# A graph-attention layer's opening in three-chunk steps: one product per chunk for h, r and s, first tile woven in, and the bias moved to x

## Chip, core and metric

One NeuronCore of a Trainium2 chip runs the whole program. The metric is the device time of one execution in microseconds (us); lower is better. PE is TensorE, DVE is VectorE, ACT is ScalarE, POOL is GpSimd, and SP is the SyncE, whose queue issues most DMAs. ACT issues some DMAs too, on a queue of its own.

## What is computed

Everything is float32. `x` has 3327 rows of 128, `adj` is 3327 x 3327 with entries 0 and 1 and ones on the diagonal. Two layers follow each other, each with a residual sum and a layer norm.

```
# layer 0
h = x @ W.T + b;  s = h @ a_s;  r = h @ a_r
e = leaky_relu(adj * s + adj * r.T, 0.2)
x1 = layernorm(x + softmax(where(adj > 0, e, -9e15), axis=1) @ h)
# layer 1: 8 features per head, 128 heads, each attends over all 3327 rows
q, k, v = (x1 @ W.T).reshape(128, 3327, 8)  for Wq, Wk, Wv
a = softmax(q @ k.T / sqrt(128) + adj + adj, axis=2)
out = layernorm(x1 + (a @ v).reshape(3327, 1024) @ Wo.T)
```

## The kernel before

**The long part, layer 1.** The 128 heads are taken in 32 groups of four. For a group, the 3327 query columns are taken in 7 blocks of 476, and the 3327 keys in 26 chunks of up to 128 (key row `p*26 + i` stands on partition `p` of chunk `i`). A block has 26 rounds, so a group has 182 and the kernel 5824. In a round PE computes scores for four head-and-chunk pairs (L135, tiles `scb` from `k4b` and `q4b`), DVE adds the adjacency to some (L1013) and ACT takes the exponential (L843), while for every third chunk ACT takes the exponential directly (L1010) and POOL multiplies by a factor made of the adjacency (L1011). Four rounds later PE multiplies with the values (L813, `av` from `e` and `v4b`). Adjacency tiles `at` hold three chunks (a stretch) and are loaded three stretches ahead by `want_adj` (L776); `make_factor` (L799) turns a tile's first chunk into POOL's factor in the first blocks.

**Between groups.** `open_group` (L735) loads the next group's `k4b` (four loads, one per head) and `v4b` (three loads) from DRAM. It is called when 28 rounds of the old group are left (`OPEN`, L852), and the seven loads are spread over these 28 rounds (L983 to L989). Before the call, `finish_to` (L949) forces whatever is left of the layer-0 tile whose rows the group needs, in one piece.

**Layer 0.** It is worked by row tiles of 128, 26 of them, by `layer0(t)` (L250). A tile needs its adjacency columns in three loads of chunks (`a`, `load_adj`), the exponentials of s for its rows (`trow`, from a table `td` in DRAM), and per chunk: weights `w` on DVE (`weigh`), their mask by `a` on POOL (`mask`, tiles 1 and up), and one PE product into an accumulator of 129 columns (`product`; the last column gives the softmax denominator). The operand `hsb` holds h scaled by an exponential of r. After the 26 products a chain follows: divide and add x (`finish`, L329), variance, an inverse root by Newton steps, scaling, a transpose to `x1T`, then q, k and v projections of 512 columns (tile 0) or 128 columns (the others), each split or copied and stored to DRAM (`qT`, `kT`, `vd`). `count` counts zeros and ones in the adjacency on DVE (L313). Tiles 1 to 25 are not done at once: their steps are put between the rounds of layer 1, a few per round, by `work_tensor` and `work` (L925, L932), in two rows: `main` (products, chain) and `aside` (weights, masks, counts). `work` runs at most one POOL step and one or no DVE step per round.

**The opening.** Before the first round everything that all tiles share and all of tile 0 is done in line (L612 to L705). In order: x is loaded; 26 transposes give `xT` (L650); seven products of 476 columns give h transposed, and DVE adds the bias b (L658); seven products give s, ACT takes the exponential and each row piece is stored to `td` (L663); 26 products with an identity that has `a_r` as a 129th column turn h back and give r (L674); two exponentials of r over all chunks (L682); POOL scales `hsb` in three pieces (L686). Then tile 0: `spread` copies a row of s to all partitions by a product (L284), 26 weights (L297), 26 products (L182), the chain. Its stores go to SP one step after they are made (`issue` and `tick`, L238), q first, then k, then v. The counts and the load of `wo` come last. Then `group` 0 is opened: q and k loads alternate between SP and ACT, v on ACT; three adjacency tiles are wanted; and tile 1's adjacency is loaded (L957 to L969). `trow` of tile 1 is loaded when the rounds have begun.

[...]

Of the kernel before, what the change touches and what calls it, by code (L numbers as in the profile page):

```python
# [8 lines left out]
F32 = mybir.dt.float32  # L9
# [38 lines left out]
def kernel(  # L48
# [76 lines left out]
    identr = const.tile([P, P + 1], F32, name="identr")  # L125
    ident = identr[:, :P]
# [17 lines left out]
    def special():  # L144
        with ExitStack() as sx, tc.manual_schedule(engines=ALL):
# [15 lines left out]
            hsb = keep.tile([P, NT, D + 1], F32, name="hsb")  # L161
            vbs = [keep.tile([P, 512 // H, H1], F32, name=f"vb{n}") for n in range(2)]
# [4 lines left out]
            ear = keep.tile([P, NT], F32, name="ear")  # L167
# [82 lines left out]
            def layer0(t, side=True, trow=None, bank=bank):  # L250
# [31 lines left out]
                def spread():  # L282
                    s["b"] = bank()
                    nc.tensor.matmul(s["b"][:, :r], one_row, trow[:, :r], start=True, stop=True)  # L284

                def weigh(n, c0, c1):
                    i0 = CH[n][0]
                    if c0 == i0:
                        s["w"][n] = bgw.tile([P, CW, 3 * T3], F32, name="w")
                    for i in range(c0, c1):  # L290
                        w, e = s["w"][n][:, i - i0, :r], er[:, i : i + 1]
                        if side:

                            w = s["w"][n][:, i - i0, :].rearrange("p (a b) -> p a b", b=T3)
                            nc.vector.tensor_scalar(w, s["t"][:, :, :T3], e, None, op0=ALU.max)  # L295
                        else:
                            nc.vector.scalar_tensor_tensor(  # L297
                                w, s["b"][:, :r], e, s["a"][n][:, i - i0, :r], op0=ALU.max, op1=ALU.mult
                            )
# [17 lines left out]
                def product(i):  # L317
# [9 lines left out]
                    )  # L327

# [50 lines left out]
                def halves(dst, c, scale):  # L379
# [13 lines left out]
                    if o + QW == 512:  # L393
                        h0 = c // 512 * 4
                        for half, sb in ((0, hi), (1, lo)):
                            at = (h0 * 2 + half if dst is qT else half * H + h0) * G + t * P * D
                            for p0, p1 in _cut(r):
                                issue(
                                    lambda at=at, sb=sb, p0=p0, p1=p1: nc.sync.dma_start(
# [5 lines left out]
                def values(c):  # L405
# [5 lines left out]
                    if c % 512 + QW == 512:  # L411
                        for p0, p1 in _cut(r):
                            at = ((t * P + p0) * D + c // 512 * (512 // H)) * H1
                            issue(
                                lambda at=at, p0=p0, p1=p1: nc.sync.dma_start(
# [6 lines left out]
                for w, dst, sc in ((wq, qT, half_scale), (wk, kT, 1.0)):  # L422
# [8 lines left out]
                main, aside = [("x", load)], [("r", load_row)] if side else [("p", spread)]  # L431
                loads = [("x", lambda n=n: load_adj(n)) for n in range(len(CH))]
                counts = []
                for n, (i0, i1) in enumerate(CH):
# [12 lines left out]
                    main.append(("n", ("W", q0 + n, 3)))  # L447
                    main += [("p", lambda i=i: product(i)) for i in range(i0, i1)] + [("t", ("P", q0 + n))]
# [163 lines left out]
            nc.vector.memset(dens, 1.0)  # L612
            nc.vector.memset(even, 0.0)
            with ExitStack() as st:
                pro = st.enter_context(tc.tile_pool(name="st_sb", bufs=1))
                pps = st.enter_context(tc.tile_pool(name="st_ps", bufs=5, space=bass.MemoryType.PSUM))
                w0 = pro.tile([P, D], F32, name="w0")
                bcol = pro.tile([P, 1], F32, name="bcol")
                ascol = pro.tile([P, 1], F32, name="ascol")
                xsb = pro.tile([P, NT, D], F32, name="xsb")  # L620
                xT = pro.tile([P, P * NT], F32, name="xT")
                hT = pro.tile([P, P * NT], F32, name="hT")
                for p0, p1 in _cut(FP):
                    nc.sync.dma_start(xsb[p0:p1], x[p0 * NT : p1 * NT, :].rearrange("(p i) d -> p i d", i=NT))
                nc.sync.dma_start(xsb[FP:P, :REST, :], x[FP * NT :, :].unsqueeze(0))
                nc.scalar.dma_start(w0, w0T)
                nc.scalar.dma_start(bcol, b0)
                nc.scalar.dma_start(ascol, a_s)
                nc.scalar.dma_start(identr[:, P : P + 1], a_r)
                nc.gpsimd.memset(hsb[:, REST:NT, :], 0.0)  # L630
                trs = [pro.tile([1, WB], F32, name=f"tr{b}") for b in range(NBLK)]
                loads, main, aside = layer0(
                    0, side=False, trow=trs[0], bank=lambda: pps.tile([P, 512], F32, tag="mm", name="mm")
                )
                for _, u in loads + main[:1]:
                    u()
                nc.sync.dma_start(wq, wqT.rearrange("k h c -> k (h c)"))
                nc.sync.dma_start(wk, wkT.rearrange("k h c -> k (h c)"))
                nc.sync.dma_start(wv, wvT.rearrange("k c h -> k (c h)"))

                def evict(n, dst, src):
                    (nc.scalar.copy if n % 2 else nc.vector.tensor_copy)(dst, src)


                xv, hv = (v.rearrange("d (p i) -> d i p", i=NT) for v in (xT, hT))
                for n, i0 in enumerate(range(0, NT, 4)):
                    pt = pps.tile([P, 4, P], F32, tag="mm", name="pt")
                    k = min(4, NT - i0)
                    for i in range(i0, i0 + k):
                        nc.tensor.transpose(pt[:, i - i0, : kr[i]], xsb[: kr[i], i, :], ident[: kr[i], : kr[i]])  # L650
                    full = sum(kr[i] == P for i in range(i0, i0 + k))
                    if full:
                        evict(n, xv[:, i0 : i0 + full, :], pt[:, :full, :])
                    if full < k:
                        evict(n, xv[:, i0 + full : i0 + k, :FP], pt[:, full:k, :FP])
                for n, (n0, _) in enumerate(blocks):
                    ph = pps.tile([P, 512], F32, tag="mm", name="ph")
                    nc.tensor.matmul(ph[:, :WB], w0, xT[:, n0 : n0 + WB], start=True, stop=True)  # L658
                    nc.vector.tensor_scalar(hT[:, n0 : n0 + WB], ph[:, :WB], bcol, None, op0=ALU.add)

                for b, (n0, _) in enumerate(blocks):
                    pr = pps.tile([P, 512], F32, tag="mm", name="pr")
                    nc.tensor.matmul(pr[:1, :WB], ascol, hT[:, n0 : n0 + WB], start=True, stop=True)  # L663
                    nc.scalar.activation(trs[b], pr[:1, :WB], AF.Exp, scale=ALPHA - 1.0)
                    nc.scalar.dma_start(td[:, n0 : n0 + WB], trs[b])
                nc.scalar.dma_start(td[:, N:], one_row[:, : NT * P + 1 - N])

                for n, i0 in enumerate(range(0, NT, 3)):
                    pb = pps.tile([P, 512], F32, tag="mm", name="pb")[:, : 3 * (D + 1)].rearrange(
                        "p (c d) -> p c d", d=D + 1  # L670
                    )
                    k = min(3, NT - i0)
                    for i in range(i0, i0 + k):
                        nc.tensor.matmul(  # L674
                            pb[: kr[i], i - i0, :], hv[:, i, : kr[i]], identr, start=True, stop=True
                        )
                    full = sum(kr[i] == P for i in range(i0, i0 + k))
                    if full:
                        evict(n, hsb[:, i0 : i0 + full, :], pb[:, :full, :])
                    if full < k:  # L680
                        evict(n, hsb[:FP, i0 + full : i0 + k, :], pb[:FP, full:k, :])
                nc.scalar.activation(er, hsb[:, :, D], AF.Exp, scale=1.0 - ALPHA)  # L682
                nc.scalar.activation(ear, hsb[:, :, D], AF.Exp, scale=ALPHA)
                nc.gpsimd.memset(hsb[:, :, D : D + 1], 1.0)
                for i0, i1 in CH:
                    nc.gpsimd.tensor_tensor(  # L686
                        hsb[:, i0:i1, :],
                        hsb[:, i0:i1, :],
                        ear[:, i0:i1].unsqueeze(2).to_broadcast([P, i1 - i0, D + 1]),
                        op=ALU.mult,  # L690
                    )
                for u in aside:
                    if isinstance(u, list):
                        while main[1][0] != "t":
                            kind, f = main.pop(1)
                            if kind == "p":
                                f()
                        main.pop(1)
                    elif u[0] in "pd":
                        u[1]()  # L700
                for kind, f in main[1:] + sum((u for u in aside if isinstance(u, list)), []):
# [263 lines left out]
            for m in range(AHEAD):  # L965
                want_adj(m)
# [447 lines left out]
```

## Time and profile before

| | |
|---|---|
| three timed runs | 10145.96, 10146.45, 10153.09 us; median 10146.45 |
| the profiled execution | 10146.98 us, of which the span of the trace is 10145.2 |
| busy in the span | ACT 9978.5 us (98%), PE 9936.6 (98%), DVE 9373.0 (92%), POOL 9211.9 (91%) |
| DMA | 1730 MB, mean 171 GB/s |

All times below are us from the span's start. A timeline row has the start, the time, the engine and line, the operation, the tile written and the tiles read, and the number of instructions that the row merges; in brackets stands the engine's idle time before it and what ended it. PE records two instructions per float32 product and one per transpose. `PEld` are weight loads, which lie under the products. A row of the stretches has, for each engine, the busy time and the number of instructions, then the granted PE clock as a share of full speed, the busy share of the DMA engines, and GB/s. An engine name with `q` is its queue of DMA issues. An idle engine costs nothing unless it is the one that sets the pace.

### The profile page before, as it was taken

The page shows a single profiled execution, that of the slowest core. Times are in us where ns is not written, and L with a number is a line of the kernel's source. Part 1 is how long each engine was busy: PE and PEld are TensorE (multiplying, and loading weights), DVE is VectorE, ACT ScalarE, POOL GpSimd, SP SyncE. Part 2 cuts the span into 40 slices and gives each one's busy share as a digit, 9 for nine tenths or more (in the row PEclk, how much of TensorE's full clock was granted, in tenths as well). Part 3 has the DMA queues.
Part 4 walks back from the last instruction along what each step waited for, and adds up shares of the span by engine and source line. Part 5 has one row for each costly group of instructions (what it writes and reads, how often), then busy time and mean ns, then how long its engine had stood idle before and what let it go on. Part 6 is the DMA issues. An engine that isn't in the chain of part 4 may idle for free.

```text
span 10145.2 us, 212048 instructions
## 1 busy us (share of the span) xinstructions
PE 9936.6 (98%) x81993; PEld 3855.0 (38%) x81993; DVE 9373.0 (92%) x11597; ACT 9978.5 (98%) x8311; POOL 9211.9 (91%) x4395
## 2 busy tenths in 40 slices
PE   7999999999999999999999999999999999999998
PEld 3333333333333333333333333333333333333333
DVE  6999999999989999989999999999999999998887
ACT  6999999999999999999999999999999999999998
POOL 6999999999999999989999999999999999998997
PEclk8999999999999999999999999999999999999999
DMA  6655555555555555555555565555555555555553
GB/s 174 200 177 166 176 170 174 172 170 173 177 162 175 178 158 176 176 168 172 168 170 175 173 182 166 159 173 175 173 178 164 163 177 175 172 162 168 165 166 121
DMA packets 1183195, 1730.00 MB, mean 171 GB/s; under 512 B 131326, under 2 KB 1170783, under 8 KB 1177949
## 3 DMA queue, kind: packets, MB, share of 16 engines
q1 hardware_dynamic: 1180810, 1714.81, 56.4%
q8 instruction: 645, 10.57, 0.4%
q14 instruction: 377, 3.09, 0.1%
q10 hardware_dynamic: 1363, 1.53, 0.1%
HBM read 1611.93 MB, written 103.95 MB: 169 GB/s over the span
## 4 chain that ended last, share of the span: by engine, by line
PE 79%; ACT 12%; DVE 4%; issue 2%; POOL 2%; DMA 1%; SPq 0%; DVEq 0%; ACTq 0%; POOLq 0%
PE av L813 40%; PE scb L135 33%; ACT e L843 6%; ACT e L1010 6%; PE bank L224 4%; DVE e L1013 3%; POOL e L1011 2%; DVE o L822 1%; PE bank L472 0%; DMA at<-ftd 0%; DMA at<-in_adjT_dram 0%; POOL at L803 0%; PE mm L182 0%; PE pb L674 0%; DMA k4b<-kT 0%
## 5 line engine op out<-in xcount | busy, mean ns | idle before, releaser
L1011 POOL TENSOR_TENSOR e<-e,at 128x952 f32<-128x952 f32 x4032 | 8969.4, 2238 | 818.0 <-ACT e L1010 739.4
L1013 DVE TENSOR_TENSOR e<-scb,at 128x952 f32<-128x952 f32 (+1 forms) x7616 | 8417.8, 1144 | 647.3 <-PE scb L135 333.0
L843 ACT ACTIVATE e<-e 128x1904 f32<-128x1904 f32 (+2 forms) x4256 | 6886.4, 1624 | 16.3 <-DVE e L1013 15.5
L813 PE MATMUL av<-e,v4b 128*32 128x476 f32 x46592 | 5872.4, 572 | 42.1 <-DVE o L822 27.8
L135 PE MATMUL scb<-q4b,k4b 32*128 32x476 f32 (+1 forms) x23296 | 4351.5, 592 | 116.8 <-ACT e L1010 36.1
L135 PEld LDWEIGHTS scb<-q4b,k4b 32*128 32x128 f32 (+1 forms) x23296 | 2533.6, 295 | 4788.8 <-issue 2642.1
L1010 ACT ACTIVATE e<-scb 128x952 f32<-128x952 f32 x4032 | 3882.0, 963 | 67.9 <-PE scb L135 37.7
L813 PEld LDWEIGHTS av<-e,v4b 128*32 128x32 f32 x46592 | 1056.6, 108 | 1068.5 <-issue 616.1
L224 PE MATMUL bank<-hsb,w 128*32 128x129 f32 (+1 forms) x5200 | 278.0, 286 | 0.0
L313 DVE TENSOR_SCALAR_CACHE_REDUCE dump<-a 128x384 bf16<-128x384 f32 (+2 forms) x468 | 247.2, 528 | 0.6
L295 DVE TENSOR_SCALAR w<-trow,er 128x129 f32<-128x129 f32 x650 | 201.1, 338 | 13.6 <-DMA trow<-td 13.6
L304 POOL TENSOR_TENSOR w<-w,a 128x384 f32<-128x384 f32 (+3 forms) x225 | 207.3, 921 | 0.1
L224 PEld LDWEIGHTS bank<-hsb,w 128*32 128x32 f32 (+1 forms) x5200 | 102.4, 108 | 148.3 <-issue 147.9
L822 DVE COPY o<-av 128x476 f32<-128x476 f32 x224 | 146.0, 652 | 7.5 <-PE av L813 6.7
L389 DVE SCALAR_TENSOR_TENSOR lo<-bank,hi 128x128 fp32r<-128x128 f32 (+1 forms) x400 | 116.6, 292 | 13.8
L386 DVE TENSOR_SCALAR hi<-bank 128x128 fp32r<-128x128 f32 (+1 forms) x400 | 112.2, 281 | 0.0
L224 PE MATMUL bank<-wv,x1T 128*32 128x128 f32 x1600 | 86.1, 287 | 5.6 <-DVE vb L408 5.6
L224 PE MATMUL bank<-wo,ot 128*32 128x128 f32 (+1 forms) x1664 | 88.8, 290 | 0.4 <-DVE ot L481 0.4
L224 PE MATMUL bank<-wq,x1T 128*32 128x128 f32 x1600 | 85.2, 285 | 0.0
L224 PE MATMUL bank<-wk,x1T 128*32 128x128 f32 x1600 | 85.2, 285 | 0.0
L472 PE MATMUL bank<-identr,o 128*128 128x128 f32 (+1 forms) x234 | 54.6, 308 | 11.0 <-DMA o<-oT 8.3
L408 DVE COPY vb<-bank 128x128 f32<-128x128 f32 (+1 forms) x200 | 56.2, 281 | 6.4 <-PE bank L224 6.4
(110 smaller groups left out, 667.5 us busy)
## 6 DMA issues: line engine op xcount, KB each, us to landing
at<-in_adjT_dram SPq DMA_DIRECT2D x1736, 476.0 KB
at<-ftd SPq DMA_DIRECT2D x1953, 238.0 KB
q4b<-qT SPq DMA_DIRECT2D x1788, 29.8 KB
k4b<-kT SPq DMA_DIRECT2D x126, 415.9 KB
at<-in_adjT_dram SPq DMA_DIRECT2D x217, 208.2 KB
at<-in_adjT_dram SPq DMA_DIRECT2D x56, 714.0 KB
a<-in_adjT_dram SPq DMA_DIRECT2D x50, 504.0 KB
ftd<-at SPq DMA_DIRECT2D x63, 238.0 KB
```

Of the source, the lines that this page charges most:

```text
L135: nc.tensor.matmul(dst, k4[32 * j : 32 * j + H4, i::NT], q4[32 * j : 32 * j + H4, :nb], start=True, stop=stop,)
L224: nc.tensor.matmul(dst[c0:c1], w[:, c0:c1], mov, **kw)
L295: nc.vector.tensor_scalar(w, s["t"][:, :, :T3], e, None, op0=ALU.max)
L304: nc.gpsimd.tensor_tensor(w, w, s["a"][n][:, c0 - i0 : c1 - i0, :r], op=ALU.mult)
L313: nc.vector.tensor_scalar(z, a, float(k), None, op0=ALU.is_equal, op1=ALU.add, accum_out=even[:, t, at : at + 1])
L389: nc.vector.scalar_tensor_tensor(lo[:r, o : o + QW], s["b"][:r, :QW], scale, hi[:r, o : o + QW].bitcast(F32), op0=ALU.mult, op1=ALU.subtract,)
L813: nc.tensor.matmul(s.av[32 * j : 32 * j + 32, :], s.v4[:r, j, i * H1 : i * H1 + 32], e[:r, j, :], start=(s.left == NT - 1), stop=(s.left = ...
L822: nc.vector.tensor_copy(o4, s.av)
L843: nc.scalar.activation(e, e, AF.Exp, scale=2.0)
L1010: nc.scalar.activation(eh, z[:r, :, :WB], AF.Exp, scale=2.0)
L1011: nc.gpsimd.tensor_tensor(eh, eh, ah, op=ALU.mult)
L1013: nc.vector.tensor_tensor(eh, z[:r, :, :WB], ah, op=ALU.add)
```

## The change

- The bias leaves h. h is now `x @ W.T` alone; b is added to the tile's rows of x on POOL (`biased`), for tile 0 ahead of the chain and for each other tile ahead of its last eight products. (The softmax weights sum to one, so b passes through the weighted sum unchanged.)
- r and s become two more columns of W: `w0` gets `W.T @ a_r` and `W.T @ a_s`, by two small products at the start, and one product of 130 columns per chunk of x gives h, r and s (`linear`). b's share in r and s is put in as a bias of ACT's exponentials. ACT, not POOL, scales `hsb`, chunk by chunk.
- x is loaded in two halves, after tile 0's rows. Three chunks at a time are transposed (`turn`), multiplied a step later, weighed for tile 0, and multiplied for tile 0 two steps after that.
- Tile 0's row of s (`t0`) is computed by itself, from its transposed rows, on all partitions. The table `td` is stored by columns after the last step.
- All tiles project k, then q, then v. Tile 0's k stores stay on SP; its q and v stores are kept in a list (`held`) and issued on ACT when the whole chain has been issued; the counts come after that.
- The first three adjacency tiles are loaded early, behind the weights. At group 0 the four k loads go to SP, q and v loads to ACT. `trow` of tile 1 is loaded ahead of its adjacency, and `wo` after it.
- `OPEN` is 18 instead of 28 rounds.

The diff, cut to its core:

```diff
-                main, aside = [("x", load)], [("r", load_row)] if side else [("p", spread)]
+                main, aside = [("x", load)], [("r", load_row)] if side else []
...
+                    if i1 == NT:
+                        main.append(("m", biased))
                     main += [("p", lambda i=i: product(i)) for i in range(i0, i1)] + [("t", ("P", q0 + n))]
...
+                def biased():
+                    nc.gpsimd.tensor_tensor(s["x"][:r], s["x"][:r], brow[:r], op=ALU.add)
...
-                for w, dst, sc in ((wq, qT, half_scale), (wk, kT, 1.0)):
+                for w, dst, sc in ((wk, kT, 1.0), (wq, qT, half_scale)):
...
+                nc.scalar.dma_start(w0[:, :D], w0T)
+                nc.scalar.dma_start(acol[:, 0:1], a_r)
+                nc.scalar.dma_start(acol[:, 1:2], a_s)
+                nc.scalar.dma_start(bcol, b0)
+                nc.scalar.dma_start(brow, _ap(b0, 0, [[0, P], [1, D]]))
+                first["load"]()
...
+                for m in range(AHEAD):
+                    want_adj(m)
...
+                nc.tensor.transpose(b[:, :D], w0[:, :D], ident)
+                nc.vector.tensor_copy(w0t, b[:, :D])
+                b = mm()
+                nc.tensor.matmul(b[:, 0:2], w0t, acol, start=True, stop=True)
+                nc.tensor.matmul(b[:, 4:6], bcol.to_broadcast([P, P]), acol, start=True, stop=True)
...
+                def turn(cs):
+                    b = pps.tile([P, 4, P], F32, tag="mm", name="mm")
+                    for i in cs:
+                        nc.tensor.transpose(b[:, i - cs[0], : kr[i]], xsb[: kr[i], i, :], ident[: kr[i], : kr[i]])
+                    for i, k, r in parts(cs):
+                        nc.vector.tensor_copy(xT[:, i : i + k, :r], b[:, i - cs[0] : i - cs[0] + k, :r])
+
+                def linear(cs):
+                    b = mm()[:, : 3 * (D + 2)].rearrange("p (c d) -> p c d", d=D + 2)
+                    for i in cs:
+                        nc.tensor.matmul(b[: kr[i], i - cs[0], :], xT[:, i, : kr[i]], w0, start=True, stop=True)
+                    for i, k, r in parts(cs):
...
+                        nc.scalar.activation(
+                            er[:r, i : i + k], v[:, :, D], AF.Exp, scale=1.0 - ALPHA, bias=bias[:r, 0:1]
+                        )
...
+                    for i in cs:
+                        nc.scalar.mul(hsb[: kr[i], i, :D], b[: kr[i], i - cs[0], :D], hsb[: kr[i], i, D : D + 1])
+                    for i in cs:
+                        first["weigh"][i]()
+
+                for n in range(len(three) + 3):
+                    if n < len(three):
+                        turn(three[n])
+                    if 1 <= n <= len(three):
+                        linear(three[n - 1])
+                    if n >= 3:
+                        for i in three[n - 3]:
+                            first["product"][i]()
...
+                for f in first["chain"]:
+                    f()
+                    tick(True)
+                for f in held:
+                    f()
+                for f in first["count"]:
+                    f()
...
-            OPEN = min(28, total // 2)
+            OPEN = min(18, total // 2)
...
             for j in range(HG):
-                engine = nc.scalar if j % 2 else nc.sync
-                queries[1](j, engine)
-                group[2][j](engine=engine)
+                group[2][j]()
+                queries[1](j, nc.scalar)
             for f in group[2][HG:]:
                 f(engine=nc.scalar)
-            for m in range(AHEAD):
-                want_adj(m)
+            aside.pop(0)[1]()
             for _, u in first_loads:
                 u()
+            nc.sync.dma_start(wo, woT)
             make_factor(0)
```

## The prediction

> **What bounds the kernel now.** I read the stretches first, because a change to the opening can only save time in which the engine that sets the pace is idle.
>
> ```profile
> core 0: us, PE busy (x) PEld busy (x) DVE busy (x) ACT busy (x) POOL busy (x), PEclk, DMA share, GB/s
> 0.00:86.00 86.00, 45.59 (x173) 31.98 (x173) 36.26 (x109) 14.16 (x23) 7.63 (x15) 0.83 0.54 130
> 86.00:153.00 67.00, 49.39 (x372) 18.30 (x372) 47.01 (x56) 49.59 (x42) 49.64 (x33) 0.81 0.71 199
> 153.00:390.00 237.00, 219.17 (x1862) 81.47 (x1861) 207.15 (x270) 216.13 (x177) 225.10 (x139) 0.97 0.69 202
> 2000.00:10000.00 8000.00, 7915.37 (x65470) 3064.20 (x65462) 7462.77 (x9120) 7988.58 (x6648) 7339.64 (x3446) 1.00 0.57 170
> ```
>
> From 2000 us on ACT works 7988.58 of 8000 us: nothing outside ACT moves that part. ACT idles 72 us before 86 us, 17 in the next 67 and 21 in the next 237. The change aims at the first two. The timeline shows the serial passes of the opening:
>
> ```profile
> 11.46 4.67 PE L650 MATMUL pt<-identr,xsb 128*128 128x128 f32 x24 [11.46 <-DMA xsb<-in_x_dram]
> ...
> 29.01 12.03 PE L674 MATMUL pb<-identr,hT 128*128 128x129 f32 x52
> ...
> 44.50 8.42 PE L182 MATMUL mm<-hsb,w 128*128 128x129 f32 x52 [3.06 <-POOL hsb L686]
> ...
> 52.96 0.16 DVE L334 COPY dens<-mm 128x1 f32<-128x1 f32 x1 [2.02 <-PE mm L182]
> ...
> 58.42 3.78 PE L182 MATMUL mm<-wq,x1T 128*128 128x512 f32 x4 [0.38 <-DVE x1T L363]
> ```
>
> and the end of the opening, in a later window:
>
> ```profile
> 78.06 0.60 SPq L742 DMA_DIRECT2D k4b<-kT  x1
> ...
> 86.31 1.03 PE L135 MATMUL scb<-q4b,k4b 32*128 32x476 f32 x4 [20.18 <-DMA v4b<-vd]
> ...
> 97.66 0.37 SPq L267 DMA_DIRECT2D trow<-td  x1
> ...
> 102.83 0.60 DVE L295 TENSOR_SCALAR w<-trow,er 128x129 f32<-128x129 f32 x2 [13.56 <-DMA trow<-td]
> ```
>
> The landmarks: tile 0's sums are read at 52.96, its x1T is used at 58.42, the first scores run at 86.31. Then DVE stops 13.56 us for trow, whose load stands on SP behind nine adjacency loads and was issued only at 97.66.
>
> **The front, to the end of tile 0's products.** Removed: 14 passes of L658 (5.83 us), 14 of L663 (5.75), 52 of L674 (12.03), the POOL scaling (6.08) and its wait. They stand in series with 26 transposes and 52 passes of products, 41.5 us from 11.46 to 52.96. After, three chunks at a time go through transposes, one product of 130 columns, exponentials and weights, and products behind them.
>
> When it starts: the new PE order puts a product of w0 with a_s ahead of all transposes of x, and a_s is third on ACT's queue. Small loads there are slow, as the DMA view of 2 to 8 us and SP's waits show:
>
> ```profile
> q1 hardware_dynamic: 129, 1.53, 95.6%
> q10 hardware_dynamic: 124, 0.06, 4.8%
> ```
>
> ```profile
> SPq L276 <- DMA w<-in_w0T_dram: 8.5, 1, 8.5
> ```
>
> (First packets, MB and share, then the wait in us.) The 512-byte pieces of w0 on q10 pass one for one with the 13 KB rows of x on q1: w0, issued at 0.75, landed near 10.86. [...] Two small products (four passes at half clock, 0.21 each), copies like x1T's 0.29, a transpose and the row product for t0 add 2.8: transposes begin at 12.7 (from 8.5+2.8 to 14).
>
> How long: a step of three chunks is 3 transposes, 6 product passes, 6 passes behind. The products' 52 passes show both clocks: 21 in 4.50 us from 44.5 (clock 0.50, 0.214 each), 31 in 3.42 from 49.5 (clock 1.00, 0.11 each). A step is 15x0.11 = 1.65 us at full clock, 3.2 at half. DVE has a copy near 0.56 (L642, 387 wide) and 3x0.26 (L297), 1.4 with gaps; ACT three small exponentials at up to 0.25 (L682) and three scalings near 0.28, between L682 and L642's 0.48: 1.6 with gaps. So PE sets 1.8 with hand-offs. [...] First fill 4 us, nine steps at 1.8, tail 1: end at 33.5, against 52.9. [...] The adjacency chunks wait for a_s and b to land, 1 or 2 us later than now, and still arrive ahead of their weights.
>
> **From the sums to the first scores.** The chain of L334 to L363 is unchanged: 5.4 us, so x1T stands at X = 39. In the old trace X to scores is 27.9. The last store of the first projection (q) went out at 63.59 and landed 2.71 later by the chain of waits, X+7.9; with k first, k4b can be loaded then. But q and vd stores now wait on ACT's queue until both vb copies are done (67.0, X+8.6), and in SP's new order the third k4b load carries a wait for the second, the fourth a wait for the fifth q4b load, hence for all q stores. At the 240 GB/s of 60 to 80 us: two k4b (0.83 MB) to X+13, four q stores with the third k4b (1.47 MB) to X+19.5, vd and q4b to X+23, fourth k4b to X+26.8. That is 1 less than now: the early k buys little, its fourth load is still last. Range 24 to 30. wo and three adjacency tiles leave this stretch; they are loaded earlier, under the front (2.1 MB after 1.5 MB of weights, landed by about 30), where no one waits.
>
> **The stall at 89.** trow's load now precedes the nine. Gain 13.56, less what is late next: POOL's first mask needs the first chunk loads, the fourth adjacency tile its own; they land about X+31 and X+39, are needed at X+38 and X+42. I take 13.3, bounds 5 and 13.6.
>
> **OPEN 28 to 18.** The forced finish goes from 8 and 4 projections (rounds 154 and 336) to 6 and 6 in the new order. The trace has ACT idle 7.83 us and about 3.7 there, some 1 us a projection: zero, plus or minus 3. At the other boundaries k4b and v4b are loaded in 18 rounds (31 us) instead of 28.
>
> **Bias by POOL.** 26 adds of 128x128, at a third of L304's 921 ns: 0.35 each, 9 us if nothing hid them. ACT at 99.9% hides them outside group 0, where POOL is busy 225 of 237 us: 0.4 there. Memset of er, brow, four td stores on SP: zero, they lie beside the front; if SP were late there, x1d alone would wait behind them.
>
> **Sum.** First scores at 39+26.8 = 65.8, 20.5 earlier; stall 13.3; adds -0.4: 33.4. The profiled execution took 10146.98 (span 10145.2), the median of runs is 10146.45; taken off the median: 10113.
>
> **Rivals.** (a) As summed, 60%: 10104 to 10120.
> (b) The front is bound by something else, half clock, DVE, or late chunks: it ends at 44 to 46. For: PE idles between small pieces. Against: full clock at 29 to 41. Gain 22: 10124, 14%.
> (c) The stall only changes its name: the mask or the fourth tile comes late, as nine chunk loads now wait for q4b and v4b landings. For: these shared waits. Against: four rounds of slack. Gain 20.5+5: 10121 and, with the fourth k4b at X+31 besides, 10126; 16%.
> (d) It does not do what it says, an earlier front that the loads eat up: (b) with the fourth k4b at X+33, 6 later, gain 16: 10130, 6%.
> (e) Slower: 18 rounds are too few at the 31 group boundaries. v4b's last piece goes out 3 rounds before the group, its first reader 4 rounds after: 12 us. Past a landing of 12 us, each further us costs 31; at more than 13.1 us on average the whole gain is gone, at 14 the time is 10113+62 = 10175. Against: DMA share 0.57 leaves room; SP's loads of the next tiles have 15 us of slack. 4%.
>
> **Chances.** A measurement of this kernel tells 0.2% (20 us) from no change: below 10126 lie (a), (b) and most of (c), 0.87; within 0.2%, (d) and the rest of (c), 0.09; slower, (e), 0.04. Range 10104 to 10127.
>
> **What would show it.** Right: transposes of x from about 12 to 13 us, dens read near 34, first scores near 66, no DVE wait over 2 us for trow, ACT idle in the first 86 us down from 72 us to about 46. Wrong: PE at clock 0.5 in 20 to 34 us, scores over 30 us after x1T, POOL waiting for an adjacency load in the first ten rounds, or ACT idle over 1 us near group starts after the second.

## The result, and the profile after

| | before | after |
|---|---|---|
| timed runs, median | 10147.7 us (six, 10145.96 to 10153.09) | 10105.25 us (six, 10103.96 to 10105.86) |
| ratio, 95% interval | | 0.9957 (0.9947 to 0.9967) |
| profiled execution, its span | 10146.98, 10145.2 us | 10105.34, 10103.5 us |

The changed kernel is 42.4 us faster where 33.4 were forecast. That is within the range, but only 1.25 us from its lower end (10104). The stretches of its profile, cut where its stages lie (the first exponential of the scores runs at 62.5 us, the first block of group 0 ends at 115):

```profile
core 0: us, PE busy (x) PEld busy (x) DVE busy (x) ACT busy (x) POOL busy (x), PEclk, DMA share, GB/s
0.00:62.00 62.00, 28.15 (x155) 21.74 (x155) 30.48 (x108) 17.18 (x64) 2.30 (x12) 0.80 0.77 206
62.00:115.00 53.00, 49.78 (x371) 17.71 (x371) 47.12 (x56) 49.48 (x42) 49.13 (x32) 0.88 0.79 222
115.00:405.00 290.00, 273.91 (x2250) 101.06 (x2253) 255.71 (x328) 269.54 (x223) 279.01 (x173) 0.96 0.70 205
2000.00:10000.00 8000.00, 7909.64 (x65404) 3058.47 (x65404) 7461.78 (x9110) 7986.49 (x6649) 7347.12 (x3468) 1.00 0.57 170
```

ACT's idle time ahead of the scores is 45 us in a stretch of 62, in the next stretch 3.5 instead of 17, and the long middle is what it was (7986.49 of 8000 us). The front, in the timeline of PE and of DVE (rows of the kernel after):

```profile
7.33 0.56 PE L755 MATMUL mm<-acol,w0t 128*128 128x2 f32 x2 [3.81 <-DMA acol<-in_a_s_dram]
...
9.60 1.49 PE L778 MATMUL mm<-ident,xsb 128*128 128x128 f32 x6
...
19.25 0.49 PE L778 MATMUL mm<-ident,xsb 128*128 128x128 f32 x3
...
20.92 0.49 PE L778 MATMUL mm<-ident,xsb 128*128 128x128 f32 x3
```

```profile
14.68 0.88 DVE L294 SCALAR_TENSOR_TENSOR w<-t,er,a 128x128 f32<-128x128 f32 x3 [2.99 <-ACT er L788]
...
28.70 0.16 DVE L335 COPY dens<-bank 128x1 f32<-128x1 f32 x1 [1.02 <-PE bank L183]
```

PE waits for a_s until 7.33, the transposes of x begin at 9.60, a step takes 1.67 us (20.92 less 19.25), and the sums are read at 28.70 instead of 52.96. (Two of the expectations below mean the next row, DVE's reciprocal, when they put the sums at 28.9; here it is the row at 28.70, as in the kernel before.) DVE's 2.99 us ahead of its first weights is laid to ACT's er, which was done at 12.8; what came last is the first adjacency chunk, whose last packets land at 14.54. Then the timeline around the first scores:

```profile
34.30 2.93 PE L183 MATMUL mm<-wk,x1T 128*128 128x512 f32 x3 [0.38 <-DVE x1T L364]
...
56.32 0.58 SPq L268 DMA_DIRECT2D trow<-td  x1
56.42 0.74 PE L134 MATMUL scb<-q4b,k4b 32*128 32x476 f32 x1 [15.10 <-DMA q4b<-qT]
61.72 0.85 PE L134 MATMUL scb<-q4b,k4b 32*128 32x476 f32 x3 [4.56 <-DMA k4b<-kT]
62.53 0.96 ACT L1049 ACTIVATE e<-scb 128x952 f32<-128x952 f32 x1 [19.62 <-PE scb L134]
...
63.73 0.59 DVE L292 TENSOR_SCALAR w<-trow,er 128x129 f32<-128x129 f32 x2
```

x1T is used at 34.30. One score runs at 56.42, the other three wait for the fourth k4b (landed at 61.67) until 61.72. DVE's weights of the next tile (L292) have no wait in front of them: the 13.56 us are gone.

Where the 41.7 us between the two spans lie, by landmarks of the two timelines:

| stretch | before | after | gain |
|---|---|---|---|
| start to the first exponential of scores | 87.6 | 62.5 | 25.1 |
| from there to the end of group 0's first block | 65.5 | 52.6 | 12.9 |
| the rest of group 0 | 291.8 | 289.4 | 2.4 |
| group 1 | 316.1 | 317.3 | -1.2 |
| groups 2 to 31 | 9356.4 | 9354.4 | 2.0 |
| after the last block | 27.8 | 27.3 | 0.5 |

Of the 8.3 us by which the spans differ by more than 33.4, some 4.6 lie ahead of the first exponential (25.1 where 20.5 to the first scores were forecast) and 3.7 behind the first block, where nothing was forecast.

### The profile page after: what moved, and what is told of

The parts are those of the page before. It is cut to its first block, busy times and chain, and to the rows that moved or that the text cites. A ratio compares the mean times of both kernels' runs of the same rounds, so it can differ in the third digit from the quotient of the medians.

```text
span 10103.5 us, 212078 instructions
## 1 busy us (share of the span) xinstructions
PE 9915.1 (98%) x81971; PEld 3840.4 (38%) x81971; DVE 9371.2 (93%) x11596; ACT 9978.5 (99%) x8352; POOL 9212.9 (91%) x4416
## 4 chain that ended last, share of the span: by engine, by line
PE 78%; ACT 13%; DVE 4%; issue 2%; POOL 2%; DMA 1%; SPq 0%; ACTq 0%; DVEq 0%; POOLq 0%
PE av L853 40%; PE scb L134 33%; ACT e L883 7%; ACT e L1049 6%; PE bank L225 4%; DVE e L1052 2%; POOL e L1050 2%; DVE o L862 1%; DMA at<-in_adjT_dram 0%; DMA at<-ftd 0%; PE bank L485 0%; POOL at L697 0%; DVE ot L494 0%; DMA a<-in_adjT_dram 0%; DVE w L292 0%
## 5 line engine op out<-in xcount | busy, mean ns | idle before, releaser
L292 DVE TENSOR_SCALAR w<-trow,er 128x129 f32<-128x129 f32 x650 | 201.2, 339 | 0.0
L485 PE MATMUL bank<-ident,o 128*128 128x128 f32 (+1 forms) x234 | 54.6, 308 | 10.4 <-DMA o<-oT 7.6
```

## The experiments

Twelve kernels were run, with the kernel before beside each; its median was 10147.8 to 10149.9 us there, so times of different sets can be compared to about 2 us. My theory was the prediction's sum; the rivals were that the step of the front is not PE's, that other loads would have covered the wait for trow, that OPEN or the adds carry the extra gain, and that the stretch to the scores is bound by the order of stores and not by bytes.

**The front: PE's step, and what starts it.** A kernel that does each transpose of x twice:

```diff
+                        for again in range(2):
-                        nc.tensor.transpose(b[:, i - cs[0], ...
+                            nc.tensor.transpose(b[:, i - cs[0], ...
```

> The changed kernel with every transpose of x in the front done twice, into the same place: three more passes a step on PE, nothing more elsewhere. Theory (once it runs, a step of 1.67 us is PE's: fifteen passes of 0.11): steps of 2.0 us, over the six or so steps that no load delays, and the sums 2 to 3 us later, at 31 to 32; time 10107 to 10108. Rival (the step is bound by DVE's or ACT's round of copies, exponentials and weights): steps stay at 1.67 and the sums at 28.9, time 10105.

Measured: 10109.05 us (10104.46 to 10109.12). PE's rows of that kernel:

```profile
17.97 0.82 PE L779 MATMUL mm<-ident,xsb 128*128 128x128 f32 x6
...
19.96 0.82 PE L779 MATMUL mm<-ident,xsb 128*128 128x128 f32 x6
...
21.96 0.82 PE L779 MATMUL mm<-ident,xsb 128*128 128x128 f32 x6
```

The step is 2.00 us instead of 1.67: three passes of 0.11 more, and the whole of it is seen. The step is PE's. The sums came 1.9 us later, at 30.62; 0.4 of that is the first weights, which began at 15.12 in this profile instead of 14.68.

The second kernel brings the small loads and the first adjacency chunk forward:

```diff
-                nc.scalar.dma_start(w0[:, :D], w0T)
                 nc.scalar.dma_start(acol[:, 0:1], a_r)
-                nc.scalar.dma_start(acol[:, 1:2], a_s)
-                nc.scalar.dma_start(bcol, b0)
-                nc.scalar.dma_start(brow, _ap(b0, 0, [[0, P], [1, D]]))
+                nc.scalar.dma_start(w0[:, :D], w0T)
+                nc.sync.dma_start(acol[:, 1:2], a_s)
+                nc.sync.dma_start(bcol, b0)
...
+                    first["loads"].pop(0)()
                 for f in first["loads"]:
                     f()
+                nc.sync.dma_start(brow, _ap(b0, 0, [[0, P], [1, D]]))
```

> The changed kernel with the loads of its opening in another order: a_s and b go to SP ahead of tile 0's rows of x, a_r goes ahead of w0 on ACT, the row of b goes to SP behind the adjacency chunks, and the first adjacency chunk goes ahead of the second half of x. In the changed kernel the transposes of x start at 9.60 us and the sums are read at 28.89; between the two DVE waits 3 us, to 14.68, for the first adjacency chunk. Theory (the front is gated at its start by these two arrivals, and by PE after them): transposes at about 7.5, first weights at about 11.5, sums at about 26.5, and 2.4 us off the end, 10103. Rival (the loads of the front take their bytes' time whatever their order, so that the second half of x or the later chunks come late instead): sums at 28 to 29, the time within 1 us of the changed kernel's, 10105.

Measured: 10104.22 us (10102.71 to 10105.83), sums at 27.04, span 10101.9. Rows of its timeline:

```profile
8.79 1.51 PE L779 MATMUL mm<-ident,xsb 128*128 128x128 f32 x6 [1.74 <-DMA xsb<-in_x_dram]
...
12.32 0.88 DVE L294 SCALAR_TENSOR_TENSOR w<-t,er,a 128x128 f32<-128x128 f32 x3 [1.42 <-ACT er L789]
```

Both arrivals moved (first weights at 12.32 instead of 14.68), but the first half of x took the place of a_s: it now lands 1.7 us later, at 8.7, and PE waits for it. Of 2.4 us that I had expected 1.7 came at the sums and 1.6 at the end; the time alone, 1 us under the changed kernel's, would not have told the two theories apart.

**The stall for trow.** One part undone: trow is loaded behind the nine adjacency loads again.

```diff
-            aside.pop(0)[1]()
```

> The changed kernel (10105.25 us) with one part undone: trow of tile 1 is loaded, as before the change, when the rounds have begun, behind the nine adjacency loads, wo, the fourth adjacency tile and xrow. Theory (what stands ahead of the first rounds moves the end one for one, and the old 13.6 us stall was this load alone): DVE's first weight waits for trow again; first scores stay at 61.7, trow is issued near 69 and lands near 75, wanted at 64: 11 us, 10116 (10112 to 10120). Rival (the stall was already covered by others: the fourth k4b load, the mask's chunk loads): 10105 to 10108.

Measured: 10115.36 us (10113.59 to 10117.8). The waits of the first 120 us have the row again:

```profile
DVE w L292 <- DMA trow<-td: 11.7, 1, 11.7
```

The stretch of the first block is 64.0 us long instead of 52.6: the stall is back, and the other loads would not have hidden it. The first exponential is 2.7 us later besides. The first adjacency chunk landed at 15.36 in this profile, 0.8 us later than in the changed kernel's. PE stood idle for 2.00 us behind it and then worked at a granted clock of 0.50, which cost about 1.6 us more at the sums:

```profile
17.50:20.80 3.30, 3.30 (x18) 3.30 (x17) 2.02 (x6) 1.35 (x6) 0.00 (x0) 0.50 1.11 256
18.00 1.50 PE L183 MATMUL bank<-hsb,w 128*128 128x129 f32 x6
```

In the changed kernel such a row takes 0.83 us. The timed runs, 10 us over the changed kernel, are the better measure of trow.

**The tiles of adjacency for the rounds.** Here they are loaded last, behind the nine adjacency loads of tile 1. This is later than before the change, where they stood ahead of these:

```diff
-                for m in range(AHEAD):
-                    want_adj(m)
...
             for _, u in first_loads:
                 u()
+            for m in range(AHEAD):
+                want_adj(m)
```

> The changed kernel with one part undone: the first three tiles of the adjacency for the score rounds (2.2 MB) are loaded behind the loads of group 0, the next tile's trow and chunks, as before the change (there they were ahead of the chunks). Theory (the stretch from the projections to the scores is bound by what its loads carry, and the early loads cost nothing under the front): the first tile lands behind nine chunk loads, near 75, the first factor and so the first products of exponentials with it come some 10 us later, and the time is 10113 to 10118. Rival (four rounds of slack and five buffers cover it): within 3 us of the changed kernel, 10105 to 10108.

Measured: 10115.69 us (10112.2 to 10119.57). Its timeline:

```profile
64.55 0.96 ACT L1049 ACTIVATE e<-scb 128x952 f32<-128x952 f32 x1 [0.87 <-PE scb L134]
...
72.64 0.59 POOL L697 TENSOR_SCALAR at<-at 128x476 f32<-128x476 f32 x1 [19.19 <-DMA at<-in_adjT_dram]
...
75.49 1.79 ACT L881 ACTIVATE e<-e 128x1904 f32<-128x1904 f32 x1 [9.98 <-DVE e L1052]
```

The first exponential stands where it did (62.7), but POOL's factor and DVE's first addition of the adjacency wait for the tile until 72.6, and ACT waits 9.98 us for that addition. With trow early and these tiles behind the nine loads, 10 us are lost; in the kernel above it is trow that is behind them, with the same loss. Each kernel undoes one move, and neither puts the tiles back where they were before the change. There they hardly held anything up, as the kernel before shows (its first exponential runs at 87.61):

```profile
88.08 0.59 POOL L803 TENSOR_SCALAR at<-at 128x476 f32<-128x476 f32 x1 [10.40 <-DMA at<-in_adjT_dram]
```

So trow had to come out from behind the nine loads, and the tiles must not go behind them. What loading the tiles under the front gains over their old place was not tried.

**From the projections to the scores.** Three kernels. In the first, tile 0's q and v stores go on SP as in any other tile; in the second, q is projected first besides; in the third, v4b's loads go on SP behind k4b's besides that.

```diff
-                first = layer0(0, side=False, trow=t0, bank=next_bank, held=held)
+                first = layer0(0, side=False, trow=t0, bank=next_bank)
```

> The changed kernel with one part undone: tile 0's q and v stores go out on SP as soon as they are made, not on ACT after the whole chain; k stays first. Theory (the first scores wait for the fourth k4b load, which waits for the fifth q4b load, and this for q stores that begin late and run beside the first k4b loads): the q stores land 8 to 9 us earlier, the fourth k4b is issued near x1T+15 instead of x1T+21.4, first scores 5 to 7 us earlier: 10099 (10097 to 10101). Rival (this stretch is bound by its 5 MB, so the order of stores does nothing): 10105, with first scores at x1T+27.

```diff
-                for w, dst, sc in ((wk, kT, 1.0), (wq, qT, half_scale)):
+                for w, dst, sc in ((wq, qT, half_scale), (wk, kT, 1.0)):
```

> As e2, and q is projected and stored ahead of k, as before the change. Theory (not the order of k and q but the late q stores hold the scores up): k stores land near x1T+11.6, q4b loads are done by then, four k4b loads follow at about 1.7 us each: first scores near x1T+21, 10099 (10097 to 10102), within 2 us of e2. Rival (k first is what keeps this stretch no longer than before the change): first scores at x1T+28 or later, 10106 or more.

```diff
             for f in group[2][HG:]:
-                f(engine=nc.scalar)
+                f()
```

> Tile 0 projects q first, all its stores go on SP, and v4b's three loads (0.47 MB) go on SP behind the four of k4b, instead of on ACT beside them. With q first and the stores on SP alone, the first exponential stood at 62.1 and the DMA engines were full from 50 to 62 us at about 195 GB/s. Theory (this stretch is bound by its bytes: the fourth k4b load shares the engines with v4b): the fourth k4b lands 0.47 MB / 0.2 MB per us = 2.3 us earlier, the first exponential at about 59.8, the end 2 us earlier, 10101.5. Rival (k4b's own rate or the landing time of its queue bounds it): first exponential at 62, the time 10103.5 to 10105.5.

Measured: 10103.55 (10102.36 to 10104.46), 10103.7 (10101.33 to 10105.1) and 10102.84 us (10101.52 to 10104.29); first exponentials at 63.1, 62.1 and 59.0 us. In the first two, my theory of the stores' order failed: k first or q first, ACT or SP, the first exponential comes 27 to 29 us after x1T. The timelines of the second and the third kernel:

```profile
46.44 5.28 SPq L636 DMA_DIRECT2D k4b<-kT  x4
48.63 4.22 ACTq L642 DMA_DIRECT2D v4b<-vd  x3
...
62.09 0.96 ACT L1049 ACTIVATE e<-scb 128x952 f32<-128x952 f32 x1 [18.62 <-PE scb L134]
```

```profile
46.35 3.27 SPq L636 DMA_DIRECT2D k4b<-kT  x4
52.08 1.64 SPq L642 DMA_DIRECT2D v4b<-vd  x3
...
58.98 0.96 ACT L1049 ACTIVATE e<-scb 128x952 f32<-128x952 f32 x1 [15.51 <-DMA a<-in_adjT_dram]
```

k4b's loads begin at the same time; with v4b's 0.47 MB behind them instead of beside them, the first exponential runs 3.1 us earlier (2.3 were expected by the bytes). Rows of two stretches, of the changed kernel first and of the second kernel below it:

```profile
50.00:54.00 4.00, 0.00 (x0) 0.00 (x0) 3.06 (x12) 0.00 (x0) 0.62 (x2) 0.50 0.74 218
54.00:58.00 4.00, 0.74 (x1) 0.29 (x1) 0.00 (x0) 0.00 (x0) 0.17 (x1) 0.50 0.37 77
```

```profile
50.00:54.00 4.00, 0.00 (x0) 0.00 (x0) 3.60 (x14) 0.00 (x0) 0.14 (x1) 0.50 0.99 203
54.00:58.00 4.00, 0.00 (x0) 0.00 (x0) 0.00 (x0) 0.00 (x0) 0.66 (x2) 0.50 1.12 198
```

In the changed kernel the DMA engines are not full here: their share is 0.74 and then 0.37, since the fourth k4b load is held until the fifth q4b load has landed (55.69). So there the wait sets the length. In the second kernel the fourth k4b goes out at 51.15, 4.6 us sooner, but takes 10.0 us to land instead of 6.0, on engines that are full at about 200 GB/s (in the first kernel it goes out at 52.06 and takes 10.1): behind the wait stand the bytes, and taking the wait away gains hardly anything. In the third kernel the fourth k4b goes out 2.1 us sooner still (49.02) and lands 9.0 us later. How much of its 3.1 us is v4b's bytes and how much the earlier issue was not separated. The gain in the time itself, about 1 us, is inside the spread.

**OPEN.** 28, as before, and 8:

```diff
-            OPEN = min(18, total // 2)
+            OPEN = min(28, total // 2)
```

> The changed kernel with OPEN at 28 rounds again. Theory (the boundaries have room either way; what changes is the forced piece of layer 0 in groups 0 and 1, where the old count was 8 and 4 projections, the new one 6 and 6): within 3 us, 10103 to 10108; group 0's end about 2.4 us later, group 1 as much shorter. Rival (loading k4b and v4b in 18 rounds costs something at each of the 31 boundaries, or saves something): over 5 us either way, spread evenly over the groups.

> The changed kernel with OPEN at 8 rounds instead of 18, to find where the slower rival of the prediction would begin. In the changed kernel's trace the fourth k4b load of a group lands 15.5 to 23.2 us (mean 19.4) and the last v4b piece 6.3 to 15.7 us ahead of the copy of the last block's output; the next group's first scores run some four rounds and a half, 8 us, ahead of that copy. With 8 rounds the fourth k4b is issued six rounds later, 10.3 us, and v4b's last piece one round later. Theory (the landing decides): k4b's mean margin of 11 us falls to about 1, so that near half of the 31 boundaries wait 1 to 3 us: 20 to 50 us in all, 10125 to 10155. Rival (the loads land faster when they go out closer together, or the rounds' own slack covers it): 10103 to 10110.

Measured: 10111.78 us (10106.82 to 10114.41) and 10134.88 us (21 runs, 10131.59 to 10142.9). ACT's idle time at the two forced finishes is 7.83 and 3.69 us before the change, 5.09 and 5.17 after it, 7.65 and 3.44 with 28. That is 1 us; the profile with 28 has 2.5 us in group 0, 1.1 the other way in group 1, and about 4 spread over the thirty later groups, which I could not lay to a row. So the theory for 28 missed: its median is 6.5 us over the changed kernel's (4.4 if each is taken against its own runs of the kernel before), not within 3.

With 8 the time is in the range that I had put down, but only in part for its reason. The span is 29.1 us longer. 3.9 lie in the rest of group 0, 7.1 in group 2 and about 10 in groups 3 to 30. In group 2 a fourth k4b load issued at 1020.5 lands at 1034.6, among tile loads:

```profile
1034.61 0.49 PEld L134 LDWEIGHTS scb<-q4b,k4b 32*128 32x128 f32 x3 [5.24 <-DMA k4b<-kT]
...
1035.48 0.96 ACT L1049 ACTIVATE e<-scb 128x952 f32<-128x952 f32 x1 [5.60 <-PE scb L134]
```

Waits for k4b of more than half a microsecond are at 5 of the 31 boundaries, not near half. 17.4 us lie behind the last block, which I had not thought of: the closing tests of the ranges (L549 to L603) no longer fit in the rounds and run after them. The last group gives about half of that back: it takes 309.6 us instead of 318.7, and ACT is idle in it for 0.6 us instead of 8.7. That it is shorter because the tests have left it is likely, but was not tried.

**The bias adds.** Tiles 1 to 25 without them (b is then left out of those rows):

```diff
-                    if i1 == NT:
-                        main.append(("m", biased))
```

> The changed kernel without the bias adds of tiles 1 to 25 on POOL (the output then lacks b there; b is zero in these inputs, so the values are the same). Theory (the adds lie under ACT, 0.4 us in all): 10104 to 10106. Rival (POOL, busy over 90 %, hands each add on): up to 25 x 0.35 = 9 us less, 10096.

Measured: 10102.74 us (10099.86 to 10105.28), a little less than the theory's 10104. The later groups take the same time (311.62 us in the mean of groups 4 to 30, 311.58 with the adds). The profile differs in group 1, by 2.8 us. There the second forced finish leaves ACT idle for 2.19 us instead of 5.17 (first row with the adds, second without):

```profile
686.43 0.96 ACT L1049 ACTIVATE e<-scb 128x952 f32<-128x952 f32 x1 [5.17 <-PE scb L134]
```

```profile
683.24 0.96 ACT L1047 ACTIVATE e<-scb 128x952 f32<-128x952 f32 x1 [2.19 <-PE scb L134]
```

No add runs near 681 us, so POOL's time is not it. In the list of work an add stands ahead of its tile's last eight products and takes its turn there, which can move them by a round; that this leaves one piece more for the forced finish is argued from the code, and wasn't tried. The rival of 9 us is out.

**The edits together.** The first has the diff of the early front and the three diffs of the stretch to the scores; the second has one line more:

> Two edits together: the loads of the opening as in the front_early kernel (1.6 us off the span there), and q first, all tile 0's stores on SP and v4b behind k4b as in the v_behind kernel (first exponential 3.5 us earlier). Theory (they lie in different stretches and add up): first exponential at about 57.5, 5 us ahead of the changed kernel's, time 10100 to 10101. Rival (the end varies more by the last group, 316 to 320 us, than these give): 10102 to 10105.

```diff
-            OPEN = min(18, total // 2)
+            OPEN = min(12, total // 2)
```

> The kernel before this one in the list with OPEN at 12 rounds instead of 18. The fourth k4b then goes out four rounds later (6.8 us of its 11 us of margin) and v4b's last piece one round later. Theory (from 28 to 18 rounds the first two groups gained 1 to 4 us by fewer forced projections, and the margin still holds): within 2 us of the one before, 10098 to 10102. Rival (some boundaries have less than the mean margin and wait): 31 x 0.3 to 1 us, 10110 to 10130.

Measured: 10099.43 us (10096.89 to 10103.61), ratio to before 0.9953 (0.9939 to 0.9966), and 10105.61 us (10105.44 to 10107.21). The first has the lowest median of all that was run, 5.8 us under the changed kernel; its first exponential runs at 56.0. With 12 it is 8.6 us ahead when the last block ends (10059.2 against 10067.8), and loses 17.3 after it. 7.0 of the 8.6 are the last group, 309.3 us long instead of 316.3, so that moving the tests out of it costs some 10 us net. Rows of its timeline behind the last block:

```profile
10077.47 1.04 POOL L555 TENSOR_TENSOR ot<-wq 128x512 f32<-128x512 f32 x1 [20.08 <-PE bank L225]
10081.67 1.86 PE L560 MATMUL bank<-ot,ones 128*1 128x512 f32 x2 [4.32 <-DVE x L520]
```

These are the closing tests, 20 us in line with nothing beside them; with 18 rounds they lie under the last group. No boundary wait of any size is left with 12. So what stops a smaller number than 18 first is where the tests end up, and the landing of k4b only after that. The time missed both ranges that were put down (10098 to 10102, or 10110 and more).

## Why the prediction was right, and where its terms were off

The mechanisms of the large terms were right: the serial passes gone, the stall gone, the fourth k4b last. How the front begins was wrong, and sizes were off, nearly all the same way: nothing cancelled, and the time came close to the end of the range.

- **The front** was the largest miss: sums at 33.5 forecast, 28.7 seen, 4.8 us more gain. (The terms put down add up to 33.9.) Two terms failed. The first is the arrival of a_s: the start at 12.7 takes it to land at about 10, which no run shows; 7.19 was seen. The 10 was my estimate from the one-for-one counts of the kernel before, by which a_s would pair with the second half of x. The DMA rows of the changed kernel from 3 to 5 us and from 5 to 6 us (packets, MB, share), and a wait of SP:

```profile
q1 hardware_dynamic: 91, 0.59, 89.6%
q10 hardware_dynamic: 80, 0.00, 2.5%
```

```profile
q1 hardware_dynamic: 47, 0.13, 42.6%
q10 hardware_dynamic: 296, 0.00, 28.4%
```

```profile
SPq L736 <- DMA acol<-in_a_r_dram: 3.5, 1, 3.5
```

  As long as the first half of x lasts, small and large packets pass about one for one (91 on q1 and 80 on q10 from 3 to 5 us), as in the kernel before (129 and 124 from 2 to 8). But the second half was not on the queue: its loads wait for the landing of a_r, 3.5 us in the row above, until 7.04. So from 5 to 6 us only 0.13 MB of q1 stood against a_s, and 296 packets of q10 passed. The forecast left out that SP's own loads of x wait for landings as well.

  So the transposes began 3.1 us sooner than forecast. Not all of that reached the sums, since another thing said there failed: the first adjacency chunk does not arrive ahead of its weights. In the ten profiles with this order of loads the first weights begin 0.13 to 0.14 us after the chunk's last packet (14.5 to 15.8), though the transposes begin anywhere from 9.6 to 11.1; in eight of them the sums follow these weights by 14.0 us (the other two are the doubled transposes and the half clock above). Where the chunk is early, in the kernel with the two edits together, the sums follow the transposes by 17.8 us:

```profile
8.22 1.51 PE L779 MATMUL mm<-ident,xsb 128*128 128x128 f32 x6 [1.15 <-DMA xsb<-in_x_dram]
...
26.06 0.16 DVE L335 COPY dens<-bank 128x1 f32<-128x1 f32 x1 [1.02 <-PE bank L183]
```

  Forecast were 20.8 (12.7 to 33.5), and this length is the second term that failed: nine steps of 1.67 for 1.8 are 1.2 us less, the rest lies in the fill and the tail. So about 3.0 of the 4.8 us are the shorter front, and 1.8 the earlier a_s, after the wait for the chunk has taken 1.3 of its 3.1 back.
- **Half clock** (rival b) did not decide. The passes of PE follow each other by 0.21 us until 13.7 and by 0.11 after that, so here a front built of short pieces held full speed, as the 1.8 us a step of the forecast took it to. PE's wait behind the chunk was 1.57 us and left the speed as it was; one of 2.00 us, in the kernel with the late trow, was followed by 3.4 us at a granted clock of 0.50. In the kernel before, the granted clock was 1.00 from 29 to 41 us, and 0.50 from 44.5 to 49, behind the wait of 3.06 us for POOL.
- **x1T to the scores**: 26.8 us forecast, 27.4 seen to the three scores at 61.72. The step was right that the fourth k4b decides and that k first buys little, and right that it would be issued only after the fifth q4b landed (55.69 and 55.71). Undoing that order gained hardly anything all the same, because the bytes stand close behind the wait. One thing said there is wrong: wo is not loaded earlier but later (issued at 66.87), where no one waits for it either.
- **The stall for trow**: 13.3 forecast; ACT's idle time in that stretch fell by 13.9 and the stretch by 12.9. The term holds only as long as the tiles of adjacency for the rounds do not come behind the nine loads in their turn: there they cost 10 us again.
- **OPEN, zero plus or minus 3**, and **the adds, -0.4**: behind the first block 3.7 us were gained, where the two terms gave -0.4. By the idle rows 1.3 are the forced finishes, with the adds' 3 us already in them. Group 0 gained 2.4 and group 1 lost 1.2. With OPEN at 28 the median is 6.5 us worse, beyond the 3 that I had allowed. The adds' cost was in the wrong place: a turn in the list, by the code, and not POOL's time.
- **Rivals c and d** are out by the timeline (no wait takes the place of trow's). **Rival e**, too few rounds, has its place right and its point wrong: at 18 k4b lands about 11 us and v4b at least 6 us ahead of its first reader, and what ends first with fewer rounds is the room for the closing tests (at 12; at 8 waits for k4b come too).

What stays open: 2 us of the gain in groups 2 to 31, and the same groups' 4 us with OPEN at 28; what the tiles of adjacency gain by their early place; and the shares of bytes and of issue in v4b's move. The last group alone takes 316 to 320 us in profiles of kernels that share its code, so that differences of 2 to 4 us in it say little.

## What to carry to other kernels

Put the loads that the first rounds need ahead of those that only later rounds need, all of them: trow behind the nine loads of tile 1 cost 10 us, and so did the tiles of adjacency, each with the other one early. Before a wait in the order of loads is removed, look at the DMA share beside it. It was 0.37 here while the fourth k4b was held, but behind the wait stood bytes for nearly the same time, and only taking other bytes out of its way brought 3 us. When you forecast when a load lands, read which of the loads around it can be on their queues at that time. When a knob shifts background work, look at the end of the span too: what finds no room before the last round is done there with nothing beside it, less what the last round's group gains by being rid of it (17 and 7 to 9 us here).

## What the runs showed of the hardware that was not expected

- In one stretch of full DMA share (0.99 to 1.12, the kernel with q first on SP) the engines moved about 200 GB/s, with k4b, q4b and v4b rows and one adjacency load in flight; between 13.7 and 30.7 us of the changed kernel, with x, adjacency and weights, 277 GB/s at a share of 0.92.
- Loads of 4 bytes a row that were issued at 1.2 us or later, beside x on the other queue, landed at 7.0 to 7.4 us in the changed kernel's profile; in the kernel with the early front a_s and a_r, issued at 0.75 ahead of x, landed at 2.8 to 3.0.
- The fourth k4b load of a group took 4.6 to 5.3 us from issue to landing at the first eleven boundaries of the changed kernel, and 9 to 14 us at the same ones with OPEN at 8, where it runs among other loads (14 for the one issued at 1020.5).
- PE's granted clock fell to 0.50 after an idle time of 2.00 us in the front of the kernel with the late trow (17.4 to 20.9 us, 0.21 us a pass), and did not after one of 1.57 us in the changed kernel's. No limit is shown by these two.
